# Beginning attention with half of the channels while the other half is still being measured

## Chip, cores and metric

The kernel runs on one core of a Trainium2 chip. The metric is the device time of one execution in microseconds (us). The engines are named as in the profile: PE (matrix products; PEld is its loading of weights), DVE (vector), ACT (scalar), POOL (GpSimd) and SP (which issues DMAs). Each engine has its own queue and works it in order; semaphores tie the queues together.

## What is computed

Four layers follow one another on a tensor of 512 channels by 64 x 64 pixels: an attention, two gated convolutions and a linear attention. Each takes its input through a group normalization and adds its result to it. Only the first matters here:

```python
x = x + _L0_conv_ref(_gn(x), wq, wk, wv, wo)

def _gn(v, G=32, eps=1e-5):          # groups of 16 channels, over all pixels
    m = mean of the group; s = variance of the group
    return (v - m) / sqrt(s + eps)

q = conv1x1(fmap, wq, gain_in); k = conv1x1(fmap, wk, gain_in); v = conv1x1(fmap, wv, gain_in)
sim = -(AA[:, :, None] + AA[:, None, :] - 2.0 * qk) * scale     # AA = sum(q * q)
out = softmax(sim) @ v
```

A group has 16 channels, so the statistics of channels 0 to 255 don't depend on those of 256 to 511.

## The kernel before

X, the input, lies in SBUF as four chunks of 128 channels by 4096 pixels, in eight blocks of 512 pixels. `trunk_kernel` loads it block by block (L171), chunks 0 and 2 by SP's queue and 1 and 3 by ACT's, 32 transfers of 256 KB. `_attention_pairs` then has DVE measure all 32 blocks (`bn_stats`, L568) and calls `_Norm.params` for all four chunks at once: DVE aggregates the statistics of a chunk (L95), PE multiplies with the mask `gmask`, which gives the mean of each group (L124), DVE makes `less`, the negative mean (L125), and the variance (L127 to L129), PE applies the mask again (L132), `known()` starts the shift of X's first block by the mean (`_Centered.take`, L383 on ACT and L385 on POOL or DVE), and DVE and ACT make the reciprocal root (L134 to L141). The reciprocal goes, as `gains` (L594, L595), into the weights instead of X (`_Centered.scaled`, L391 on ACT, L395 elsewhere).

`project(pair)` computes q, k and v for two heads (pair 0 and 2: also v for the next two). It works on two blocks of pixels at a time and is a loop of four rounds, k = 0 to 3. Each round has a "turned" half (`_SevenTurned`, the values v: X is the stationary operand, 16 matmul instructions of 128 columns in a product) and a direct half (`_Seven`, q and k: 4 instructions of 512 columns in a product). Each half uses a scheme of seven products where eight would be plain (`_Seven.steps`): sums of weights made once (`sums`, L441) and differences of blocks of X made each round (`differences`, L454), in four pairs that depend on one another in order. The steps come in the order p1, p5, p2, p7, p6, p3, p4. p1 multiplies chunks 0 and 1 of the first block with the first half of a weight, p2 chunks 2 and 3 with the second half. Both accumulate in one bank of PSUM, the memory that PE writes:

```python
def p1():
    add(0, a[:, 0:2], [x(c, 0) for c in range(2)], True)
    kept[0] = keep(0, ps[0])
def p2():
    add(0, a[:, 2:4], [x(2 + c, 0) for c in range(2)], False)
    put(0, 0, ps[0], None)
```

`keep` is an ACT copy to SBUF (L664), since p1 alone enters other sums too. `put` takes a result out: an ACT copy where nothing is added (L682), a DVE addition otherwise (L684). The additions of p7 and p6 into the kept sums are DVE's (L490, L494). At each round's end the squares of q are summed by PE (L671, tile ps_a). In round 0 of pair 0 the differences are pinned to program order on DVE.

PSUM banks for p1 and p5 come from a pool of three double banks (tag "s"), which the mask products (gn_ps), ps_a and later the scores share. Weights of pair 0 are loaded by SP inside `project` (L611), behind X in its queue. After pair 0's projection the attention of that pair begins (L745), then the other pairs, then the other layers.

The order of each engine's queue is made by a planner: it takes instructions by their place in the program where they are ready by its own estimate of time. `keep_in_program_order` pins an instruction behind the one traced before it on the same engine. The planner may move unpinned ones ahead: `step_b` (L1186), a small subtraction of the second layer that needs only the vector of biases, stands before the first statistic on DVE.

Of the kernel before, what the change touches and what calls it, by code (L numbers as in the profile page):

```python
# [10 lines left out]
FP = mybir.dt.float32  # L11
# [5 lines left out]
P = 128  # L17
# [4 lines left out]
BLK = 512  # L22
# [75 lines left out]
class _Norm:  # L98
# [3 lines left out]
    def __init__(self, nc, small, gmask, mv=None):  # L102
        self.nc, self.small, self.gmask = nc, small, gmask
        self.less = self.tile("less", NC)
        self.r = self.tile("r", NC)
        self.mv, self.given = mv, mv is not None
        if mv is None:
            self.mv = small.tile([P, NC, 2], FP, tag="gn_mv", name="gn_mv")

# [3 lines left out]
    def params(self, c0, c1, stats, bank, known=lambda: None):  # L113


        nc, n, mv, gmask = self.nc, c1 - c0, self.mv, self.gmask
        less, r = self.less[:, c0:c1], self.r[:, c0:c1]
        d, a, s, t = (self.tile(f"{v}{c0}", n) for v in "dast")
        if not self.given:
            for c in range(c0, c1):  # L120
                _aggregate(nc, mv, stats, c)
        yield
        ps = bank()
        nc.tensor.matmul(ps[:, 0:n], gmask, mv[:, c0:c1, 0], start=True, stop=True)  # L124
        nc.vector.tensor_scalar(less, ps[:, 0:n], -1.0, None, ALU.mult)  # L125

        nc.vector.tensor_add(d, mv[:, c0:c1, 0], less)  # L127
        nc.vector.tensor_mul(d, d, d)
        nc.vector.tensor_add(d, d, mv[:, c0:c1, 1])  # L129
        yield  # L130
        ps = bank()
        nc.tensor.matmul(ps[:, 0:n], gmask, d, start=True, stop=True)  # L132
        known()
        nc.vector.tensor_scalar(a, ps[:, 0:n], GN_EPS, None, ALU.add)  # L134
        nc.scalar.activation(s, a, AF.Sqrt)
        nc.vector.reciprocal(r, s)

        nc.vector.tensor_mul(t, r, r)
        nc.vector.tensor_mul(t, t, a)
        nc.vector.tensor_scalar(t, t, -0.5, 1.5, ALU.mult, ALU.add)  # L140
        nc.vector.tensor_mul(r, r, t)  # L141


def _all(pieces):
    for _ in pieces:
        pass
# [13 lines left out]
def trunk_kernel(ctx: ExitStack, tc: tile.TileContext, a: dict, out: bass.AP):  # L160
# [4 lines left out]


    X = base.tile([P, NC, N], FP, tag="X", name="X")
    for b in range(NB):
        for c in range(NC):
            eng = nc.sync if c % 2 == 0 else nc.scalar  # L170
            eng.dma_start(out=X[:, c, ts(b, BLK)], in_=a["x"][c, :, ts(b, BLK)])  # L171

    vec = base.tile([P, NVEC], FP, tag="vec", name="vec")
    nc.gpsimd.dma_start(out=vec, in_=a["vecs"])
# [38 lines left out]
    ]  # L213
    Z = dram.tile([NB, BLK], FP, tag="Z", name="Z")

    stats, mv = _attention(tc, a, X, ident, gmask, neg2, small, new_stats, centered)

    stats, norm = _gated_convs(tc, a, X, vcol, vall, gmask, small, new_stats, centered, stats, mv, F)
    _linear_attention(tc, a, X, vcol, vall, ident, gmask, small, centered, stats, norm, F3, Z, out)
# [134 lines left out]
class _Centered:  # L354
# [25 lines left out]
    def take(self, xs, c, eng=None):  # L380
        less = self.less[:, c : c + 1]
        if eng is None:
            self.nc.scalar.activation(xs, xs, AF.Identity, bias=less)  # L383
        else:
            eng.tensor_scalar(xs, xs, less, None, ALU.add)  # L385

    def scaled(self, w, rstd, eng, c0=0, c1=NC, pinned=False):

        if eng is self.nc.scalar:
            for c in range(c0, c1):  # L390
                eng.activation(w[:, c], w[:, c], AF.Copy, scale=rstd[:, c : c + 1])  # L391
# [28 lines left out]
class _Seven:  # L420
# [39 lines left out]
                skip_group_check=not first,  # L460
            )

    def steps(self, a, b, s, t, x, bank, keep, put, early=lambda more, last: None):

        nc = self.nc
        ps, kept = {}, {}

        def add(j, w, hs, first):  # L470

            if first:
                ps[j] = bank(j)
            self.multiply(ps[j], w, hs, first)

        def p1():
            add(0, a[:, 0:2], [x(c, 0) for c in range(2)], True)
            kept[0] = keep(0, ps[0])

        def p5():  # L480
            add(1, s[0], t[0], True)
            kept[1] = keep(1, ps[1])

        def p2():
            add(0, a[:, 2:4], [x(2 + c, 0) for c in range(2)], False)
            put(0, 0, ps[0], None)

        def p7():
            add(2, s[2], t[2], True)
# [36 lines left out]
SUM_LOW, SUM_HIGH = 1e-20, 1e30  # L526


def _attention_pairs(tc, a, X, QO, gmask, small, centered, stats, mv, okay):

# [18 lines left out]
    with tc.tile_pool(name="att1", bufs=1) as p1, tc.tile_pool(  # L549
# [16 lines left out]
        for b in range(NB):  # L566
            for c in range(NC):
                nc.vector.bn_stats(stats[:, c, b, :], X[:, c, ts(b, BLK)])  # L568
        norm = _Norm(nc, small, gmask)
        centered.by(norm)  # L570
        _all(
            norm.params(
                0, NC, stats, lambda: ps_mm.tile([P, BLK], FP, tag="mm", name="gn_ps"),
                centered.first(lambda c: X[:, c, 0:BLK]),
            )
        )
        rstd = norm.r


        halves = p1.tile([P, 32], FP, tag="halves", name="halves")  # L580
# [9 lines left out]
        A = p1.tile([P, NT, 2], FP, tag="A", name="A")  # L590


        gains = p1.tile([P, 2, NC], FP, tag="gains", name="gains")
        nc.vector.tensor_scalar(gains[:, 0], rstd, 2 * scale * gain_in, None, ALU.mult)  # L594
        nc.vector.tensor_scalar(gains[:, 1], rstd, gain_in, None, ALU.mult)  # L595
        seven = _Seven(tc, nc.tensor.matmul)

        turned = _SevenTurned(tc, nc.tensor.matmul)

        def home(pair):  # L600

            return V if pair % 2 else QO[NC - 1]
# [1 line left out]
        def project(pair, meanwhile=None):  # L604


            w = p1.tile([P, 3, NC, P], FP, tag="wqkv", name=f"wqkv{pair}")
            w = [w[:, n] for n in range(3)] + [p1.tile([P, NC, P], FP, tag="wo", name="wv")]
            src = [(pair, 0), (pair, 1), (pair, 2), (pair + 1, 2)][: 2 if pair % 2 else 4]
            for n, (p, m) in enumerate(src):  # L610
                nc.sync.dma_start(out=w[n], in_=a["L0_wqkv"][p][:, m])  # L611
            def scaled(n, eng, c0=0, c1=NC):
                centered.scaled(w[n], gains[:, n // 2 if n > 1 else n], eng, c0, c1, (pair, n, c0) == (0, 2, 0))

            if pair == 0:

                scaled(2, nc.vector, 0, 2)
                scaled(3, nc.scalar)
                scaled(0, nc.gpsimd)
                scaled(2, nc.vector, 2, NC)  # L620
                scaled(1, nc.scalar)
                centered.began()
            for n in range(len(src) if pair else 0):
                scaled(n, nc.gpsimd)
            Q = QO[pair]

            def matrices(t):
# [16 lines left out]
            def differences(k):  # L644
                if pair == k == 0:

                    return (
                        tc.keep_in_program_order(ins)
                        for ins in seven.differences(nc.vector, view(k), diff)
                    )  # L650
                if pair == 0:
                    for b in (2 * k, 2 * k + 1):
                        for c in range(NC if b else 0):
                            centered.take(X[:, c, ts(b, BLK)], c)
                return seven.differences(nc.vector, view(k), diff)

            def bank(j):
# [26 lines left out]
                    nc.vector.tensor_add(d, ps, more)  # L684

            late, psa = [], []
            for c in range(NC if pair == 0 else 0):
                centered.take(X[:, c, ts(1, BLK)], c)
            pieces = differences(0)
            for k in range(NB // 2):  # L690
                after = iter(())
                for g, (wa, wb, ws, sums) in enumerate(made):
# [2 lines left out]
                    steps = (turned if values else seven).steps(  # L695
                        wa, wb, ws, diff, view(k), bank, keep,
                        lambda m, n, ps, more: put(dst[m], 2 * k + n, ps, more),
                    )
                    for n, step in enumerate(steps):
                        if n == 0:  # L700
# [156 lines left out]
        nc.vector.tensor_scalar(okay, ps[0:1, 0:1], float(P), None, ALU.is_ge)  # L857


def _attention(tc, a, X, ident, gmask, neg2, small, new_stats, centered):  # L860

    nc = tc.nc
    gain_out = 1.0 / math.sqrt(C)
# [5 lines left out]
    _attention_pairs(tc, a, X, O, gmask, small, centered, stats, mv, okay)  # L869
    found = nc.values_load(okay[0:1, 0:1])  # L870
    with tc.If(found < 1, label="general"):

# [238 lines left out]
def _gated_convs(ctx, tc, a, X, vcol, vall, gmask, small, new_stats, centered, stats, mv, F):  # L1111
# [18 lines left out]
    for layer in ("L1", "L2"):  # L1130
# [55 lines left out]
        nc.vector.tensor_sub(step_b, b_in[:, :, 1], b_in[:, :, 0])  # L1186
        wsum = {}

        def more(n):
# [937 lines left out]
```

## Time and profile before

| what | value |
|---|---|
| runs | 3826.85, 3827.91 and 3833.11 us; median 3827.91 |
| profiled execution, span | 3828.3 us (TensorE clock granted: 0.996) |
| X transfers | 16 on ACT's queue, 16 on SP's; 5.4 and 5.5 us from issue to landing (median) |
| first statistic of X | 6.35 us |
| last aggregate done, gains made | 27.1, 31.6 us |
| first product of the projection | 33.06 us |
| first round ends, projection of pair 0 ends | 60.55, 136.5 us |

The page lists each engine's busy time and the span in 40 slices, one of them 96 us. The part that the change touches lies in the first slice and the beginning of the second, so it must be read from views of single stretches: the timeline (start, length, engine, line, operation, result and operands, and in brackets the idle time before and what ended it) and the table of busy times by stretch. A matmul's length in the timeline contains the pipeline; the distance between starts tells the pace.

### The profile page before, as it was taken

Reading aid. Unit: us, or ns where it says so; the run is one execution under the profiler, and the core shown is the slowest. Engines: PE = TensorE matmul, PEld = TensorE weight load, DVE = VectorE, ACT = ScalarE, POOL = GpSimd, SP = SyncE. Lnnn points to the kernel's source line nnn. Section 1 sums busy time; section 2 is a strip of 40 time slices with the busy share of each in tenths; the row PEclk is TensorE's granted clock in tenths of the full one; section 3 lists DMA queues with packets and bytes.
Section 4 is the critical chain, followed back from the end, with each engine's and each line's share of the span. In section 5 each row is a group of like instructions: output and inputs, shape, how many; then the busy total and the mean of one; then the engine's idle time right before and its main releaser. Section 6 shows DMA issues by size and latency. Waiting matters only on the chain. (4 is left out here: it accounts for less than half of the span.)

```text
span 3828.3 us, 81625 instructions
## 1 busy us (share of the span) xinstructions
PE 3752.0 (98%) x35294; PEld 1657.9 (43%) x35294; DVE 2688.1 (70%) x3242; ACT 2069.3 (54%) x2998; POOL 132.2 (3%) x112
## 2 busy tenths in 40 slices
PE   6999999999999999999999999999999999999999
PEld 5633334333365333343333334554445544455543
DVE  6577787777765777876776757766677677665437
ACT  3577774777735777746665655663246632355210
POOL 0000000000000000000000000000000000122112
PEclk9999999999999999999999999999999999999999
DMA  2000000000000000000000015772057730564312
GB/s 100 9 1 1 1 1 9 1 1 1 1 1 9 1 1 1 1 9 1 1 1 1 1 49 168 198 201 81 13 157 194 199 102 27 151 178 103 97 56 91
DMA packets 178413, 212.91 MB, mean 56 GB/s; under 512 B 13032, under 2 KB 121832, under 8 KB 177920
## 3 DMA queue, kind: packets, MB, share of 16 engines
q1 hardware_dynamic: 151232, 148.46, 14.5%
q10 hardware_dynamic: 26784, 59.11, 4.2%
q8 instruction: 280, 4.59, 0.5%
q14 instruction: 85, 0.70, 0.1%
q0 software_dynamic: 32, 0.06, 0.0%
HBM read 147.81 MB, written 59.77 MB: 54 GB/s over the span
## 5 line engine op out<-in xcount | busy, mean ns | idle before, releaser
L753 ACT ACTIVATE pt<-ps_s,A 128x512 f32<-128x512 f32 x2048 | 1286.3, 687 | 534.8 <-PE ps_s L745 527.1
L832 DVE TENSOR_TENSOR acc<-acc,pt 128x1024 f32<-128x1024 f32 x960 | 1174.1, 1223 | 327.8 <-ACT pt L753 300.8
L745 PE MATMUL ps_s<-O,K 64*64 64x512 f32 x8192 | 1111.6, 589 | 0.0
L745 PEld LDWEIGHTS ps_s<-O,K 64*64 64x64 f32 x8192 | 334.3, 133 | 553.8 <-issue 307.1
L765 PE MATMUL av<-pt,O 64*64 64x512 f32 x4096 | 558.2, 590 | 0.9 <-ACT pt L753 0.9
L765 PE MATMUL av<-pt,V 64*64 64x512 f32 x4096 | 554.4, 590 | 0.0
L1006 ACT COPY S<-S 32x1295 f32<-32x1295 f32 (+1 forms) x272 | 341.4, 1256 | 217.4 <-DMA S<-F 105.6
L765 PEld LDWEIGHTS av<-pt,O 64*64 64x64 f32 x4096 | 171.5, 133 | 276.1 <-issue 254.9
L765 PEld LDWEIGHTS av<-pt,V 64*64 64x64 f32 x4096 | 168.3, 133 | 281.0 <-issue 270.3
L933 PE MATMUL ps<-diff,w_sum 128*128 128x512 f32 x516 | 242.0, 601 | 3.1 <-DVE w_sum L441 1.9
L933 PEld LDWEIGHTS ps_cv<-S,T 64*32 64x32 f32 x13824 | 194.1, 105 | 111.5 <-issue 73.0
L933 PE MATMUL ps_cv<-S,T 64*32 64x128 f32 x13824 | 233.6, 273 | 5.0 <-issue 2.4
L933 PE MATMUL ps<-h,w_out_L 128*128 128x512 f32 x512 | 229.6, 599 | 1.5 <-DVE X L1287 1.4
L454 DVE TENSOR_TENSOR diff<-X 128x512 f32<-128x512 f32 x200 | 134.0, 683 | 83.1 <-PE ps L933 46.4
L383 ACT ACTIVATE X<-X,gn_less 128x512 f32<-128x512 f32 x122 | 77.3, 709 | 152.0 <-DVE gn_less L125 152.0
L933 PE MATMUL ps<-X,w_in_L 128*128 128x512 f32 x304 | 145.8, 611 | 10.8 <-ACT w_in_L L391 5.4
L933 PE MATMUL ps<-h,pw_L 128*128 128x512 f32 x320 | 143.8, 599 | 1.9 <-DVE h L1275 1.6
L933 PEld LDWEIGHTS ps<-h,w_out_L 128*128 128x128 f32 x512 | 94.0, 190 | 118.3 <-issue 96.5
L933 PEld LDWEIGHTS ps<-diff,w_sum 128*128 128x128 f32 x516 | 94.6, 190 | 116.8 <-issue 106.5
L454 DVE TENSOR_TENSOR diff<-X,diff 128x512 f32<-128x512 f32 x200 | 135.3, 683 | 12.9 <-PE ps L933 11.3
L1060 DVE STREAM_TRANSPOSE h<-ps_cv 128x512 f32<-128x512 f32 x112 | 109.2, 1048 | 48.6 <-PE ps_cv L933 48.2
L933 PE MATMUL ps<-agg,w_proj 128*128 128x512 f32 x256 | 118.5, 602 | 1.0 <-DVE turned L1060 0.9
(233 smaller groups left out, 3324.7 us busy)
## 6 DMA issues: line engine op xcount, KB each, us to landing
T<-in_L_T_dram SPq DMA_DIRECT2D x112, 384.0 KB, 4.6
F<-plane ACTq DMA_DIRECT2D x112, 324.0 KB, 3.5
S<-F SPq DMA_DIRECT2D x224, 162.0 KB, 4.6
S<-G SPq DMA_DIRECT2D x96, 153.0 KB, 4.3
G<-plane ACTq DMA_DIRECT2D x48, 289.0 KB, 2.5
row<-G SPq DMA_DIRECT2D x48, 272.0 KB, 3.3
T<-in_L_T_dram SPq DMA_DIRECT2D x48, 256.0 KB, 4.1
out_dram<-y SPq DMA_DIRECT2D x32, 256.0 KB, 2.0
```

The costliest lines, as they stand in the source:

```text
L383: self.nc.scalar.activation(xs, xs, AF.Identity, bias=less)
L454: yield eng.tensor_tensor(t[j][c], a(c), b(c), ALU.subtract)
L745: nc.tensor.matmul(ps[ts(half, D), ts(h, BLK)], K[rows, t * P + half * D : t * P + (half + 1) * D], QO[pair][rows, cols], start=True, stop ...
L753: exp = nc.scalar.activation(pt[:, ts(h, BLK)], ps[:, ts(h, BLK)], AF.Exp, bias=A[:, t, h : h + 1])
L765: nc.tensor.matmul(av[half][rows, :], v[keys, t * P + h * D : t * P + (h + 1) * D], pt[keys, ts(h, BLK)], start=(t == 0), stop=(t == NT - 1),)
L832: add = nc.vector.tensor_add(acc, acc if u > 1 else first, pt)
L933: self.tc.keep_in_program_order(self.nc.tensor.matmul(*args, **kw))
L1006: nc.scalar.copy(second, first)
L1060: nc.vector.transpose(out, src)
```

## The change

X is loaded in two parts: first chunks 0 and 1, on SP and ACT; then, after pair 0's four weights, chunks 2 and 3, all on SP. The statistics follow in that order, each pinned on DVE. The parameters are made twice, for chunks 0 and 1 and for 2 and 3. Within the first of these, a statistic of the second half is traced wherever the chain waits for another engine (`meanwhile`, and `pause` behind the root). Then the first halves of the weights are scaled, chunks 0 and 1 of blocks 0, 2, 4 and 6 are shifted (ACT and POOL by turns), and p1 of all four rounds, turned and direct, is done ahead (`begin`), eight products. Each result is copied by ACT into a part of QO[1], which pair 1 uses later. Four stand before the remaining statistics, three in the gaps of the second parameters, one after them. In the loop p1 takes p2's matmuls, alone in its bank, and adds the kept result on DVE; p2 does nothing. In addition ACT's root, copies and the scalings named in the diff are pinned, and `step_b` is pinned in both gated convolutions.

```diff
+    def load_x(chunks, engines):
+        for b in range(NB):
+            for c, eng in zip(chunks, engines):
+                eng.dma_start(out=X[:, c, ts(b, BLK)], in_=a["x"][c, :, ts(b, BLK)])
+
+    load_x((0, 1), (nc.sync, nc.scalar))
...
+        lambda: load_x((2, 3), (nc.sync, nc.sync)),
...
         nc.vector.tensor_scalar(a, ps[:, 0:n], GN_EPS, None, ALU.add)
-        nc.scalar.activation(s, a, AF.Sqrt)
+        self.pin(nc.scalar.activation(s, a, AF.Sqrt))
+        self.pause()
         nc.vector.reciprocal(r, s)
...
         def p1():
-            add(0, a[:, 0:2], [x(c, 0) for c in range(2)], True)
+            if p1_kept is not None:
+                kept[0] = p1_kept
+                add(0, a[:, 2:4], [x(2 + c, 0) for c in range(2)], True)
+                put(0, 0, ps[0], p1_kept)
+                return
+            ps[0] = bank(0)
+            self.first(a, x, ps[0])
             kept[0] = keep(0, ps[0])
...
         def p2():
-            add(0, a[:, 2:4], [x(2 + c, 0) for c in range(2)], False)
-            put(0, 0, ps[0], None)
+            if p1_kept is None:
+                add(0, a[:, 2:4], [x(2 + c, 0) for c in range(2)], False)
+                put(0, 0, ps[0], None)
...
+        def taken(b, c0, c1, engines=(None,)):
+            for c in range(c0, c1):
+                tc.keep_in_program_order(
+                    centered.take(X[:, c, ts(b, BLK)], c, engines[c % len(engines)])
+                )
+
+        def measure(b, c):
+            tc.keep_in_program_order(nc.vector.bn_stats(stats[:, c, b, :], X[:, c, ts(b, BLK)]))
+
+        first = [(b, c) for b in range(NB) for c in range(2)]
+        rest = [(b, 2 + c) for b, c in first]
...
+        def parameters(c0, c1, meanwhile, known):
+
+            norm.pause = meanwhile
+            for _ in norm.params(c0, c1, stats, bank_gn, known):
+                meanwhile()
+            for n, g in enumerate((2 * scale * gain_in, gain_in)):
+                nc.vector.tensor_scalar(gains[:, n, c0:c1], norm.r[:, c0:c1], g, None, ALU.mult)
...
+        for n in (2, 0, 3, 1):
+            load_w(n)
+        load_rest()
+        for at in first:
+            measure(*at)
+        parameters(
+            0, 2, lambda: measure(*rest.pop(0)), lambda: taken(0, 0, 2, (None, nc.gpsimd))
         )
-        rstd = norm.r
+        scaled_first(2, nc.scalar, 0, 2, True)
+        scaled_first(0, nc.gpsimd, 0, 2)
+        for k in range(1, NB // 2):
+            taken(2 * k, 0, 2, (None, nc.gpsimd))
...
+        def begin(n=1):
+
+            for _ in range(n):
+                k, values = to_begin.pop(0)
+                ps = ps_mm.tile([P, BLK], FP, tag="mm", name="ps7")
+                (turned if values else seven).first(
+                    w_first[2 if values else 0], lambda c, n: X[:, c, ts(2 * k + n, BLK)], ps
+                )
+                t = begun[k, values] = QO[1][:, ts(2 * k + values, BLK)]
+                tc.keep_in_program_order(nc.scalar.copy(t, ps))
+
+        begin(4)
+        for at in rest:
+            measure(*at)
+        parameters(2, NC, begin, lambda: taken(0, 2, NC, (nc.gpsimd, nc.vector)))
+        for n in (3, 1):
+            scaled_first(n, nc.scalar, 0, 2, True)
+        begin(len(to_begin))
...
             if pair == 0:
 
-                scaled(2, nc.vector, 0, 2)
-                scaled(3, nc.scalar)
-                scaled(0, nc.gpsimd)
-                scaled(2, nc.vector, 2, NC)
-                scaled(1, nc.scalar)
+                w = w_first
+                scaled_first(2, nc.vector, 2, NC, True)
+                scaled_first(3, nc.scalar, 2, NC, True)
+                scaled_first(0, nc.gpsimd, 2, NC)
+                scaled_first(1, nc.scalar, 2, NC, True)
                 centered.began()
...
+                        p1_kept=begun.get((k, values)) if pair == 0 else None,
...
-        nc.vector.tensor_sub(step_b, b_in[:, :, 1], b_in[:, :, 0])
+        tc.keep_in_program_order(nc.vector.tensor_sub(step_b, b_in[:, :, 1], b_in[:, :, 0]))
```

More of the change, by code (lines that the diff above doesn't have):

```diff
@@ L106, in __init__ @@
         self.mv, self.given = mv, mv is not None
+        self.pin = lambda ins: ins
+        self.pause = lambda: None
         if mv is None:
@@ L167, in trunk_kernel @@
     X = base.tile([P, NC, N], FP, tag="X", name="X")
[L168 to L171, printed above, removed]
+    def load_x(chunks, engines):
[3 more added lines that the diff above has]
+    load_x((0, 1), (nc.sync, nc.scalar))
     vec = base.tile([P, NVEC], FP, tag="vec", name="vec")
@@ L214, in trunk_kernel @@
     Z = dram.tile([NB, BLK], FP, tag="Z", name="Z")
-    stats, mv = _attention(tc, a, X, ident, gmask, neg2, small, new_stats, centered)
+    stats, mv = _attention(
+        tc, a, X, ident, gmask, neg2, small, new_stats, centered,
+        lambda: load_x((2, 3), (nc.sync, nc.sync)),
+    )
     stats, norm = _gated_convs(tc, a, X, vcol, vall, gmask, small, new_stats, centered, stats, mv, F)
@@ L382, in take @@
         if eng is None:
-            self.nc.scalar.activation(xs, xs, AF.Identity, bias=less)
-        else:
-            eng.tensor_scalar(xs, xs, less, None, ALU.add)
+            return self.nc.scalar.activation(xs, xs, AF.Identity, bias=less)
+        return eng.tensor_scalar(xs, xs, less, None, ALU.add)
     def scaled(self, w, rstd, eng, c0=0, c1=NC, pinned=False):
@@ L390, in scaled @@
             for c in range(c0, c1):
-                eng.activation(w[:, c], w[:, c], AF.Copy, scale=rstd[:, c : c + 1])
+                ins = eng.activation(w[:, c], w[:, c], AF.Copy, scale=rstd[:, c : c + 1])
+                if pinned:
+                    self.tc.keep_in_program_order(ins)
         else:
@@ L461, in multiply, with first, steps @@
             )
-    def steps(self, a, b, s, t, x, bank, keep, put, early=lambda more, last: None):
+    def first(self, a, x, ps):
+        self.multiply(ps, a[:, 0:2], [x(c, 0) for c in range(2)], True)
+    def steps(self, a, b, s, t, x, bank, keep, put, early=lambda more, last: None, p1_kept=None):
         nc = self.nc
@@ L526, with _attention_pairs @@
 SUM_LOW, SUM_HIGH = 1e-20, 1e30
-def _attention_pairs(tc, a, X, QO, gmask, small, centered, stats, mv, okay):
+def _attention_pairs(tc, a, X, QO, gmask, small, centered, stats, mv, okay, load_rest):
     nc = tc.nc
@@ L565, in _attention_pairs, with bank_gn @@
         nc.scalar.activation(mark, mark, AF.Sqrt)
-        for b in range(NB):
-            for c in range(NC):
-                nc.vector.bn_stats(stats[:, c, b, :], X[:, c, ts(b, BLK)])
+        def bank_gn():
+            return ps_mm.tile([P, BLK], FP, tag="mm", name="gn_ps")
+        def taken(b, c0, c1, engines=(None,)):
[3 more added lines that the diff above has]
+                )
@@ L569, in _attention_pairs @@
+        def measure(b, c):
+            tc.keep_in_program_order(nc.vector.bn_stats(stats[:, c, b, :], X[:, c, ts(b, BLK)]))
+        first = [(b, c) for b in range(NB) for c in range(2)]
+        rest = [(b, 2 + c) for b, c in first]
         norm = _Norm(nc, small, gmask)
+        norm.pin = tc.keep_in_program_order
         centered.by(norm)
[L571 to L575, printed above, removed]
-        )
@@ L577, in _attention_pairs @@
-        rstd = norm.r
+        gains = p1.tile([P, 2, NC], FP, tag="gains", name="gains")
+        def parameters(c0, c1, meanwhile, known):
[4 more added lines that the diff above has]
+                nc.vector.tensor_scalar(gains[:, n, c0:c1], norm.r[:, c0:c1], g, None, ALU.mult)
+        names = [(0, 0), (0, 1), (0, 2), (1, 2)]
+        w = p1.tile([P, 3, NC, P], FP, tag="wqkv", name="wqkv0")
@@ new lines, in _attention_pairs, with load_w, scaled_first @@
+        w = [w[:, n] for n in range(3)] + [p1.tile([P, NC, P], FP, tag="wo", name="wv")]
+        w_first = w
+        def load_w(n):
+            pair, m = names[n]
+            nc.sync.dma_start(out=w_first[n], in_=a["L0_wqkv"][pair][:, m])
+        def scaled_first(n, eng, c0=0, c1=NC, pinned=False):
+            centered.scaled(w_first[n], gains[:, n // 2 if n > 1 else n], eng, c0, c1, pinned)
+        for n in (2, 0, 3, 1):
[3 more added lines that the diff above has]
+            measure(*at)
@@ new lines, in _attention_pairs @@
+        parameters(
+            0, 2, lambda: measure(*rest.pop(0)), lambda: taken(0, 0, 2, (None, nc.gpsimd))
+        )
+        scaled_first(2, nc.scalar, 0, 2, True)
+        scaled_first(0, nc.gpsimd, 0, 2)
+        for k in range(1, NB // 2):
+            taken(2 * k, 0, 2, (None, nc.gpsimd))
+        seven = _Seven(tc, nc.tensor.matmul)
+        turned = _SevenTurned(tc, nc.tensor.matmul)
+        begun = {}
+        to_begin = [(k, values) for k in range(NB // 2) for values in (True, False)]
@@ new lines, in begin @@
+        def begin(n=1):
[4 more added lines that the diff above has]
+                    w_first[2 if values else 0], lambda c, n: X[:, c, ts(2 * k + n, BLK)], ps
+                )
+                t = begun[k, values] = QO[1][:, ts(2 * k + values, BLK)]
[3 more added lines that the diff above has]
+            measure(*at)
@@ L590, in _attention_pairs @@
         A = p1.tile([P, NT, 2], FP, tag="A", name="A")
[L593 to L598, printed above, removed]
         def home(pair):
@@ L604, in project @@
         def project(pair, meanwhile=None):
[L607 to L613, printed above, removed]
-            if pair == 0:
-                scaled(2, nc.vector, 0, 2)
-                scaled(3, nc.scalar)
-                scaled(0, nc.gpsimd)
-                scaled(2, nc.vector, 2, NC)
-                scaled(1, nc.scalar)
-                centered.began()
-            for n in range(len(src) if pair else 0):
-                scaled(n, nc.gpsimd)
+            if pair == 0:
+                w = w_first
[3 more added lines that the diff above has]
+                scaled_first(1, nc.scalar, 2, NC, True)
+                centered.began()
+            else:
+                w = p1.tile([P, 3, NC, P], FP, tag="wqkv", name=f"wqkv{pair}")
+                w = [w[:, n] for n in range(3)] + [p1.tile([P, NC, P], FP, tag="wo", name="wv")]
+                src = [(pair, 0), (pair, 1), (pair, 2), (pair + 1, 2)][: 2 if pair % 2 else 4]
+                for n, (p, m) in enumerate(src):
+                    nc.sync.dma_start(out=w[n], in_=a["L0_wqkv"][p][:, m])
+                for n in range(len(src)):
+                    centered.scaled(
+                        w[n], gains[:, n // 2 if n > 1 else n], nc.gpsimd
+                    )
             Q = QO[pair]
@@ L651, in differences @@
                 if pair == 0:
-                    for b in (2 * k, 2 * k + 1):
-                        for c in range(NC if b else 0):
-                            centered.take(X[:, c, ts(b, BLK)], c)
+                    if k:
+                        taken(2 * k, 2, NC)
+                    taken(2 * k + 1, 0, NC)
                 return seven.differences(nc.vector, view(k), diff)
@@ L686, in project @@
             late, psa = [], []
-            for c in range(NC if pair == 0 else 0):
-                centered.take(X[:, c, ts(1, BLK)], c)
+            if pair == 0:
+                taken(1, 0, NC)
             pieces = differences(0)
@@ L857, in _attention_pairs, with _attention @@
         nc.vector.tensor_scalar(okay, ps[0:1, 0:1], float(P), None, ALU.is_ge)
-def _attention(tc, a, X, ident, gmask, neg2, small, new_stats, centered):
+def _attention(tc, a, X, ident, gmask, neg2, small, new_stats, centered, load_rest):
     nc = tc.nc
@@ L868, in _attention @@
     mv = small.tile([P, NC, 2], FP, tag="mv", name="mv")
-    _attention_pairs(tc, a, X, O, gmask, small, centered, stats, mv, okay)
+    _attention_pairs(tc, a, X, O, gmask, small, centered, stats, mv, okay, load_rest)
     found = nc.values_load(okay[0:1, 0:1])
```

## The prediction

> **What bounds the kernel now.** I read the page first: PE is busy for 98% of the span, so what counts is when PE starts to have work and whether it then waits. The first of the 40 slices is the only one below 9. So I read the first 140 us: a table of stretches, the timeline, the waits and the DMA view.
>
> ```profile
> PE 3752.0 (98%) x35294; PEld 1657.9 (43%) x35294; DVE 2688.1 (70%) x3242; ACT 2069.3 (54%) x2998; POOL 132.2 (3%) x112
> PE   6999999999999999999999999999999999999999
> ```
>
> The stretches (length, then busy time of PE, PEld, DVE, ACT, POOL; the last columns are clock, DMA share and GB/s):
>
> ```profile
> 6.35:26.04 19.69, 0.00 (x0) 0.00 (x0) 19.39 (x33) 1.49 (x2) 0.00 (x0) 1.00 1.05 387
> 26.04:33.03 6.99, 1.15 (x4) 1.00 (x4) 5.05 (x21) 4.13 (x10) 2.88 (x2) 1.00 0.15 55
> 38.96:60.55 21.59, 21.59 (x121) 15.37 (x121) 12.45 (x22) 17.14 (x29) 0.00 (x0) 1.00 0.01 1
> 60.55:111.12 50.57, 50.57 (x297) 36.12 (x296) 23.45 (x37) 9.55 (x17) 0.00 (x0) 1.00 0.00 1
> ```
>
> Until 26 us DVE (statistics) and DMA (X) are both full; PE does nothing. From 26 to 33 a chain of small instructions makes means and gains. After it PE never stops. Timeline:
>
> ```profile
> 6.27 0.16 DVE L1186 TENSOR_TENSOR step_b<-vec 128x4 f32<-128x4 f32 x1 [4.35 <-DMA vec<-in_vecs_dram]
> 6.35 19.78 DVE L568 BATCH_NORM_STATS2 stats<-X 128x6 f32<-128x512 f32 x32
> ...
> 29.95 0.16 DVE L134 TENSOR_SCALAR gn_a<-gn_ps 128x4 f32<-128x4 f32 x1 [0.68 <-PE gn_ps L132]
> 31.47 0.16 DVE L595 TENSOR_SCALAR gains<-gn_r 128x4 f32<-128x4 f32 x1
> 33.06 3.76 PE L516 MATMUL ps<-wqkv,X 128*128 128x128 f32 x16 [3.15 <-ACT wv L391]
> 36.61 0.63 PE L516 MATMUL ps<-O,diff 128*128 128x128 f32 x2
> 37.04 1.92 PE L458 MATMUL ps<-X,wqkv 128*128 128x512 f32 x2
> 38.75 1.87 PE L516 MATMUL ps<-O,diff 128*128 128x128 f32 x14
> ```
>
> PE's first product starts at 33.06 and takes 3.4 us for 16 matmuls. Later ones, from PE's timeline, take 1.79 (turned, 112.91 to 114.69) and 1.72 us (direct, 126.11 to 127.83):
>
> ```profile
> 112.91 1.95 PE L516 MATMUL ps<-O,diff 128*128 128x128 f32 x16
> 114.69 1.95 PE L516 MATMUL ps<-wqkv,X 128*128 128x128 f32 x16
> 126.11 1.88 PE L458 MATMUL ps<-diff,w_sum 128*128 128x512 f32 x4
> 127.83 1.88 PE L458 MATMUL ps<-X,wqkv 128*128 128x512 f32 x4
> 136.50 0.64 PE L671 MATMUL ps_a<-sq,halves 128*32 128x256 f32 x8
> ```
>
> The loop's first round lasts 27.49 us (33.06 to 60.55), the next two 25.28 each, of which 0.57 is squares that the first lacks. So 27.49 - 24.71 = 2.8 us is lost at the start, and projection ends at 136.50.
>
> **What the Trainium skill says.** "TensorE: Matmul & The Clock Gate", "What's actually happening": PE runs at half clock until one busy window of about 3.4 us, and the window runs free of the kernel. The trace agrees: double pitch from 33.06 to 38.96, 5.9 us, hence the 2.8 lost (the granted clock in the table says 1.00 all the same). "DMA: Bandwidth & Descriptors", "Issuing engines are not separate DMA queues": SP and ACT share 16 DMA engines. Agrees: with both queues 387 GB/s; from 25.4 to 27 us, SP alone, slices of 328 to 451. "GPSIMD Engine Reference", "Specifications": POOL shares SBUF access with DVE instructions that have two SBUF inputs. Agrees: a 4-element multiply took 0.57 instead of 0.16 us beside POOL's 1.84 us shift of X. Statistics have one input, so I take them as undisturbed, an estimate.
>
> **The change part by part.**
>
> *Loads.* 256 KB at 387 GB/s is 0.68 us. The last of 32 X loads is issued at 19.90 and lands 5.4 later, so the n-th load lands near 3.4 + 0.68n. All new loads but eight go through SP, at 0.33 to 0.45 us of issue each, under 0.68: no new bound. Chunks 0 and 1 are in by n=16, 14.3 us; the four weights by 17.0 (they were last before); chunks 2 and 3 from 17.7 to 27.9 instead of 25.2. ACT is rid of eight issues.
>
> *step_b's pin.* DVE waited 4.35 us for vec before the first statistic. Now it starts with the first landing, 0.81 + 3.7 (the shortest from issue to landing in the view of tile X) = 4.5. DMA then paces it: the sixteenth ends at 15.0.
>
> *First parameters.* Two aggregates, 0.5: 15.6. Pinned behind them is a statistic of chunk 2's first block, which lands at 17.7. In-order DVE holds the mean there until 18.3 if the planner puts it ahead, and the shifts of X and the second mask product wait with it. Three small operations with 0.3 for contention: 19.1. From them to the variance 0.7 (29.26 to 29.95), the second statistic inside: 19.9. Root and third statistic: 20.6. Reciprocal to gains 1.25 (30.38 to 31.63): 21.9. First ACT scaling 0.4: **PE starts at 22.3**. Ends: 21.5 (mean ahead of the statistic), 23.5 (0.6 on each of two waits).
>
> *Eight products.* 4 x 1.79 + 4 x 1.72 = 14.0, plus the clock's start: half of 3.4 to 6.8 us, 1.7 to 3.4, I take 2.55. Two mask products for the second half stand in PE's queue, 0.5. Last early product: 22.3 + 2.55 + 14.0 + 0.5 = **39.35**. POOL's shifts (1.84 each, needed one per 3.5 us) and ACT's copies (0.59) lie beside it.
>
> *Second parameters.* DVE's 13 remaining statistics at 0.59: 21.9 + 7.7 = 29.6, aggregates 30.1. PE reaches their mask product only after the fifth early product, 22.3 + 2.55 + 8.8 = 33.6; the second mask product after the sixth, 35.6; gains 2.3 later (29.32 to 31.63), 38.0. So PE, not DVE, sets the pace, and the later landing costs nothing: its cover is the queue of products, 3.5 us thick.
>
> *Handover.* ACT's queue is pinned: copy of product 7, four scalings of 0.3, copy of product 8, then two scalings: 40.9. The sum of weights 0.4 (41.3), two differences 1.2 (42.5). The turned p1 on chunks 2 and 3 ends at 39.35 + 1.79 = 41.1: a hole of 1.4. p5 then ends at 44.3. p7, now next, needs the third pair of differences, and before these DVE does p1's add 0.6, three sums 1.1 and two other differences: 42.5 + 0.6 + 1.1 + 4 x 0.6 = 46.6: a hole of 2.3. Together 3.7. In the kernel before, the planner put half of the direct p1 into this very hole (37.04). If a whole one goes there, 1.7 is filled: **2.0** stays. Ends 0.5 and 3.7.
>
> *Rest of the loop.* Before, 136.50 - 33.06 - 2.8 = 100.6; without the early products 86.6. Eight ACT copies into the result (0.59) become DVE adds (0.69), and eight ACT copies of p1 go to the early phase. DVE is busy for 23.45 of 50.57 us in two rounds; four more adds of 0.69 make 26.2 of 43.6. I cost it at nothing, hidden by PE; if the cover fails, rival D. The other pins, the moved weight loads and the memsets: nothing, they are beside PE's work.
>
> **Sum.** 39.35 + 2.0 + 86.6 = 127.95, against 136.50: **8.55 us earlier**. After that PE is the bound in a stream that only shifts. The profiled execution spans 3828.3, 0.4 above the median of the runs (3827.9): 3828.3 - 8.55 - 0.4 = **3819.4**. What can be told from no change here is about 0.2%, 7.7 us; the forecast lies just past it. With all ends: gains of 4.8 to 11.7, so 3816.2 to 3823.1.
>
> **Rivals.**
> A. *Holes unfilled, late start*: the planner fills neither hole, PE starts at 23.5. 8.55 - 1.7 - 1.2 = 5.6: 3822.3. For it: DVE and ACT are pinned there. Against: it filled such a hole before.
> B. *All ends good*: mean goes first, clock warms soon, holes filled: gain 11: 3816.9. For: the wait for chunk 2 exists only if the planner believes it landed. Against: it needs luck in three places.
> C. *The mask product stands ahead of the early products in PE's queue.* PE then waits until 30.1 with most products undone, cools down and does them late: the end of product 8 moves from 39.35 to some 45.5: gain 2.4: 3825.5. For: the planner orders by its own times. Against: the products come first in the program.
> D. *Slower: evictions on DVE.* p1's bank is now freed by a DVE add in a queue with the differences, and with ps_a held only two such banks are left for p1 and p5. If the add stands behind a difference that waits for PE, the next block's p5 has no bank. It decides from a delay of one product plus one p1, 3.5 us; 2 us beyond that in each of eight blocks is 16: 3819.4 + 16 = 3835.4. For: DVE's queue is full after the fourth direct product. Against: per round it has about 13 of 21.8 us.
>
> **How the numbers follow.** Forecast 0.50, A 0.20, B 0.15, C 0.07, D 0.08. The forecast's own spread around 8.55 crosses 7.7: I count a tenth of it (0.05) as no change, and nothing of B. Faster 0.45 + 0.15 = 0.60, and 0.04 of A for a start in between: 0.64. No change 0.05 + 0.16 + 0.07 = 0.28. Slower 0.08. The range takes in A, B and the ends, 3815.5 to 3825.0; left out are D, most of C and tails.
>
> **What would show it.** First L516 product near 22, at double pitch for 3.4 to 6.8 us; the last early copy near 40; a few microseconds of PE gap or a direct product hoisted between 41 and 47; projection's last squares near 128; DVE's first statistic at 4.5 and a wait for DMA X between the aggregates and the mean. Wrong if: the first product comes after 25, PE waits on a mask product, or gaps of PE appear in rounds two to four.

## Result, and the profile after

The changed kernel takes 3820.44 us, the median of 7 runs (3817.9 to 3825.35); the kernel before, run beside it, 3831.18 (7 runs, 3826.85 to 3833.5). The ratio is 0.9975, 95% interval 0.9965 to 0.9985: 5.7 to 13.4 us faster. The profiled execution spans 3821.0 us, 7.3 less than that of the kernel before.

In the timeline of the changed kernel, the lines that answer to those of the prediction (start, length, engine, line, operation, tiles, and in brackets the idle time before and what ended it):

```profile
4.56 2.47 DVE L596 BATCH_NORM_STATS2 stats<-X 128x6 f32<-128x512 f32 x4 [2.64 <-DMA X<-in_x_dram]
...
15.27 0.58 DVE L95 BATCH_NORM_AGGREGATE gn_mv<-stats 128x2 f32<-128x48 f32 x2
...
17.71 0.69 DVE L596 BATCH_NORM_STATS2 stats<-X 128x6 f32<-128x512 f32 x1 [1.85 <-DMA X<-in_x_dram]
18.32 0.14 DVE L127 TENSOR_SCALAR gn_less<-gn_ps 128x2 f32<-128x2 f32 x1
...
22.51 0.80 PE L535 MATMUL ps<-wqkv,X 128*128 128x128 f32 x2 [2.41 <-ACT wqkv L398]
...
24.80 3.18 PE L535 MATMUL ps<-wqkv,X 128*128 128x128 f32 x14
```

The statistics start 1.8 us earlier. The first mean, `gn_less`, is made at 18.32 although its mask product began at 16.00: DVE stood for 1.85 us in front of the statistic ahead of it, whose block of X had not landed. PE starts at 22.51 instead of 33.06, at half pace.

The end of the early phase and the handover, on PE alone:

```profile
33.97 0.28 PE L126 MATMUL gn_ps<-gn_mv,gmask 128*128 128x2 f32 x2
...
36.05 2.03 PE L535 MATMUL ps<-wqkv,X 128*128 128x128 f32 x16
37.92 1.88 PE L467 MATMUL ps<-X,wqkv 128*128 128x512 f32 x4
39.64 1.95 PE L535 MATMUL ps<-wqkv,X 128*128 128x128 f32 x16
43.19 0.49 PE L535 MATMUL ps<-O,diff 128*128 128x128 f32 x2 [1.60 <-DVE diff L463]
43.51 1.02 PE L467 MATMUL ps<-X,wqkv 128*128 128x512 f32 x2
44.37 5.33 PE L535 MATMUL ps<-O,diff 128*128 128x128 f32 x46
...
128.00 0.64 PE L747 MATMUL ps_a<-sq,halves 128*32 128x256 f32 x8
```

Eight products lie between 22.51 and 39.64; then comes p1 of round 0, a hole of 1.76 us (p1's pace is 1.79, so 41.43 to 43.19), half of a direct p1 (43.51) as in the kernel before, and no further hole. Projection ends at 128.00 instead of 136.50. The table of stretches (length, then busy PE, PEld, DVE, ACT, POOL):

```profile
39.64:62.55 22.91, 21.31 (x121) 15.38 (x120) 17.08 (x31) 10.35 (x20) 0.00 (x0) 1.00 0.01 2
62.55:106.12 43.57, 43.57 (x257) 31.02 (x256) 25.46 (x41) 12.22 (x21) 0.00 (x0) 1.00 0.00 1
```

Rounds 1 and 2 last 43.57 us together instead of 50.57, and PE is busy throughout.

The 8.50 us are still there to a tenth when attention ends: its last exponential starts at 2212.65 instead of 2221.24, 8.59 earlier. In the layers behind it the distance wanders: 5.1 us at 2880 us, 8.1 at 3555, 7.3 at the end. So the experiments measure where projection ends, and the time of the whole kernel only where a version is to be judged.

### The profile page after: what moved, and what is told of

It is laid out like the page before. It is cut to its first block, busy times and chain, and to the rows that moved or that the text cites. A ratio compares the mean times of both kernels' runs of the same rounds, so it can differ in the third digit from the quotient of the medians.

```text
span 3821.0 us, 81661 instructions
## 1 busy us (share of the span) xinstructions
PE 3753.6 (98%) x35298; PEld 1658.8 (43%) x35298; DVE 2693.8 (70%) x3261; ACT 2063.6 (54%) x2989; POOL 138.5 (4%) x117
## 3 DMA queue, kind: packets, MB, share of 16 engines
q8 instruction: 280, 4.59, 0.5%
```

## Experiments

All numbers are starts from the trace of one profiled execution of each: the first early (or first) product, p1 of round 0 in the loop, which is where the last early product ends, p5 of round 0, and the end of projection, where the squares of its last round begin.

| run | first product | p1 in the loop | p5 | projection ends | from p1 to the end | against the change |
|---|---|---|---|---|---|---|
| before | 33.06 | | 36.61 | 136.50 | | +8.50 |
| changed | 22.51 | 39.64 | 43.19 | 128.00 | 88.36 | |
| e1: pin alone, on before | 33.09 | | 36.64 | 136.63 | | +8.63 |
| e2: none ahead | 32.78 | | 37.63 | 136.43 | | +8.43 |
| e3: old loads | 30.15 | 46.30 | 49.85 | 134.66 | 88.36 | +6.66 |
| e4: no statistics in the gaps | 20.44 | 37.54 | 41.08 | 125.90 | 88.36 | -2.10 |
| e5: two weights ahead | 21.35 | 38.14 | 41.68 | 126.50 | 88.36 | -1.50 |
| e6: PE kept busy | 22.29 | 36.99 | 40.53 | 125.35 | 88.36 | -2.65 |
| e7: ACT's order | 22.51 | 40.03 | 43.36 | 128.14 | 88.11 | +0.14 |
| e9: early shift | 22.48 | 39.83 | 42.41 | 127.16 | 87.33 | -0.84 |
| e10: early shift and ACT's order | 22.46 | 38.52 | 40.31 | 125.24 | 86.72 | -2.76 |
| e8: e5, no gaps, PE busy, e7 | 20.12 | 35.51 | 38.84 | 123.62 | 88.11 | -4.38 |
| e11: e8 and the early shift | 21.24 | 36.04 | 37.83 | 122.76 | 86.72 | -5.24 |

The last column can't be read alone. From the first product to the loop's p1 PE has the same work in the changed kernel, e4, e5, e7, e9 and e10, and yet it takes 17.13, 17.10, 16.79, 17.52, 17.35 and 16.06 us: the stretch at half pace at the start isn't equally long in each execution. A difference of 1 us in the last column can be that. The stretch from p1 to the end doesn't have this fault: it is 88.36 in all five kernels whose edit leaves the handover as it is, and equal in e7 and e8, and in e10 and e11. So an edit of the start is judged by the first product, one of the handover by this stretch. The times of whole kernels, one run each but for e8 and e11, don't help: e5's is the lowest of all, 3817.13, and e10's is 3823.52, although its projection ends 1.26 us earlier.

**e1, the pin of step_b alone**, put on the kernel before:

```diff
-        nc.vector.tensor_sub(step_b, b_in[:, :, 1], b_in[:, :, 0])
+        tc.keep_in_program_order(nc.vector.tensor_sub(step_b, b_in[:, :, 1], b_in[:, :, 0]))
```

> Kernel before with step_b's pin alone. Theory (DMA sets the end of the statistics): first statistic at 4.6 instead of 6.35 us, last one 0.3 us earlier at most, first product 32.8 to 33.1, projection of pair 0 ends at 136.2 to 136.5. Rival (DVE is the bound, the pin pays): everything 1.8 us earlier, end at 134.7.

```profile
7.53 10.57 DVE L568 BATCH_NORM_STATS2 stats<-X 128x6 f32<-128x512 f32 x16 [0.46 <-DMA X<-in_x_dram]
```

The first statistic starts at 4.59, the last at 25.48, where it was 25.45. The 1.8 us of early start are lost again to DMA: two waits for blocks of X take 0.63 of it, and for the rest the statistics follow one another more slowly, 0.66 us each in the line above against 0.6 before, close to the 0.68 at which blocks land. The pin pays nothing by itself; the rival is refuted.

**e2, no product ahead**, the rest as changed:

```diff
-        to_begin = [(k, values) for k in range(NB // 2) for values in (True, False)]
+        to_begin = []
-            for _ in range(n):
+            for _ in range(min(n, len(to_begin))):
```

> Changed kernel without the eight products ahead: p1 stays in the loop with p2, all else as changed. Theory (the products ahead are what pays): the two p1 of round 0 may still start near 22.5, as they need the first half alone; then PE waits for the second gains near 35 and for the sums, p5 near 37.7; projection ends near 138, ten later than changed and 1.5 later than before. Rival (the split of loads and statistics pays by itself): end at 128 to 130.

It ends at 136.43, as the kernel before. So the split of loads and parameters doesn't pay by itself, and on top of it the products ahead are worth all of the 8.4 us. The early start of p1 didn't come: p1 stood behind both mask products of the second half in PE's queue.

```profile
30.50 0.59 PE L126 MATMUL gn_ps<-gn_mv,gmask 128*128 128x2 f32 x2 [10.46 <-DVE gn_mv L95]
32.33 0.59 PE L134 MATMUL gn_ps<-gn_d,gmask 128*128 128x2 f32 x2 [1.24 <-DVE gn_d L131]
32.78 3.45 PE L535 MATMUL ps<-wqkv,X 128*128 128x128 f32 x16
37.63 0.49 PE L535 MATMUL ps<-O,diff 128*128 128x128 f32 x2 [1.40 <-DVE diff L463]
```

From there p1 ran beside the second parameters, at half pace, and PE then waited for p5, which came at 37.63 as expected (37.7), 1.0 later than in the kernel before. That the end is no later all the same, and most of the 1.6 us by which the guess of 138 was off, is the clock's doing: here PE was at full pace soon after p5 began, in the kernel before only from 38.96 on, and from p5 to the end it took 98.80 us instead of 99.89. At the same pace the split by itself would have cost about 1 us, an estimate from these two numbers.

**e3, X loaded as before**, products ahead as changed:

```diff
-    load_x((0, 1), (nc.sync, nc.scalar))
+    load_x(range(NC), 2 * (nc.sync, nc.scalar))
-        lambda: load_x((2, 3), (nc.sync, nc.sync)),
+        lambda: None,
```

> Changed kernel with X loaded block by block, all four chunks, by SP and ACT by turns, and the weights behind it. Theory (the load order lets the products start): first half complete at 23.8, first product near 31, projection ends near 136.5, no better than before. Rival (the order of loads hardly matters): end at 128 to 130.

First product 30.15, end 134.66: 1.8 better than before, where "no better" was expected. 0.85 of it is the start, which came that much before the 31 expected; about 1 us is the clock, as the early products took 16.15 us here and 17.13 in the changed kernel. Without the new order of loads at most 1.8 of 8.5 us are left, so loads and products ahead pay as a pair, and neither does alone.

**e4 and e5, the first mean's wait.** e4 traces no statistic of chunks 2 and 3 within the first parameters; e5 leaves it and loads two of the four weights behind X instead of all four ahead.

```diff
# e4
-            0, 2, lambda: measure(*rest.pop(0)), lambda: taken(0, 0, 2, (None, nc.gpsimd))
+            0, 2, lambda: None, lambda: taken(0, 0, 2, (None, nc.gpsimd))
# e5
-        for n in (2, 0, 3, 1):
-            load_w(n)
-        load_rest()
+        for n in (2, 0):
+            load_w(n)
+        load_rest()
+        for n in (3, 1):
+            load_w(n)
```

> Changed kernel with no statistic of chunks 2 and 3 in the gaps of the first parameters; they come after. Theory (the mean waits behind the statistic whose block lands at 17.7): mean at 16.5 instead of 18.3, first product near 21.0 instead of 22.5, projection ends near 126.5 instead of 128.0. Rival (the later statistics now end later and hold the second parameters): end at 128 or later.

> Changed kernel with only two of the four weights loaded ahead of chunks 2 and 3, the other two behind them. Theory (the mean waits for chunk 2's first block): that block lands two transfers, 1.35 us, earlier at 16.3; first product near 21.2, projection ends near 126.7. Rival (something else holds the start): no change, 128.0.

DVE in e4, then in e5:

```profile
16.46 0.16 DVE L127 TENSOR_SCALAR gn_less<-gn_ps 128x2 f32<-128x2 f32 x1 [0.74 <-PE gn_ps L126]
```

```profile
16.55 0.69 DVE L596 BATCH_NORM_STATS2 stats<-X 128x6 f32<-128x512 f32 x1 [0.59 <-DMA X<-in_x_dram]
17.16 0.14 DVE L127 TENSOR_SCALAR gn_less<-gn_ps 128x2 f32<-128x2 f32 x1
```

The mean moves from 18.32 to 16.46 and 17.16, the first product by 2.07 and 1.16, the end by 2.10 and 1.50; in e5 0.34 of the 1.50 is a shorter stretch at half pace. Theory holds in both: filling a gap of DVE with work whose data is not there yet makes the gap longer. e4's gain is 0.6 larger than expected. About half of that lies between the last aggregate and the gains, 4.24 us here (15.71 to 19.95) and 4.54 in the kernel before, where DVE also shifted a block of X; the rest wasn't followed up. What the rival feared didn't happen: without the stall DVE ends the second half's last aggregate at 30.21, where it was 30.50, although it has three statistics more to do after the gains. PE reaches their mask product at 31.87.

**e6, PE kept busy before the start.** 14 products of the mask with a block of X, whose result nobody reads:

```diff
+        spare = ps_av.tile([P, BLK], FP, tag="av0", name="spare")
+        turns = [9, 0, 3, 2]
+
+        def turn_over():
+            for _ in range(turns.pop(0)):
+                tc.keep_in_program_order(
+                    nc.tensor.matmul(spare, gmask, X[:, 0, 0:BLK], start=True, stop=True)
+                )
+        turn_over()
...
-            0, 2, lambda: measure(*rest.pop(0)), lambda: taken(0, 0, 2, (None, nc.gpsimd))
+            0, 2, lambda: (measure(*rest.pop(0)), turn_over()), lambda: taken(0, 0, 2, (None, nc.gpsimd))
```

> Changed kernel with 14 products of the mask with X, whose result nobody reads, on idle PE before the first early product. Theory (half clock costs 2.6 us at the start): early products at full pace from 22.5, the last ends near 37.0 instead of 39.6, projection ends near 125.4. Rival (the next bound, the second statistics near 30.5, takes most of it): end at 127 to 128.

```profile
19.72 1.96 PE L634 MATMUL spare<-X,gmask 128*128 128x512 f32 x4
22.29 2.18 PE L535 MATMUL ps<-wqkv,X 128*128 128x128 f32 x16 [0.61 <-ACT wqkv L398]
24.31 1.88 PE L467 MATMUL ps<-X,wqkv 128*128 128x512 f32 x4
```

The first product takes 2.0 us, where it took 3.4 at half pace in the kernel before; the last early one ends at 36.99, projection at 125.35. The 2.6 us are there: 2.43 from the early products (14.70 us instead of 17.13) and 0.22 from a first product that starts earlier. The second statistics don't take them back.

**e7, ACT's order at the handover.**

```diff
-        for n in (3, 1):
-            scaled_first(n, nc.scalar, 0, 2, True)
+        scaled_first(3, nc.scalar, 0, NC, True)
+        scaled_first(1, nc.scalar, 0, 2, True)
         begin(len(to_begin))
...
-                scaled_first(3, nc.scalar, 2, NC, True)
```

> Changed kernel with ACT's scaling of the second half of one weight ahead of the copy of the last early product. Theory (ACT's pinned order makes the hole of 1.7 us between p1 and p5): sum of weights 1.1 us earlier, hole 0.4, projection ends near 126.7. Rival (the next pair of differences makes a hole of its own): end at 127.7 or 128.0.

A miss: 128.14, or 0.25 gained from p1 to the end where 1.3 had been expected. ACT and DVE of this run show why:

```profile
40.76 0.57 ACT L652 COPY O<-ps 128x512 f32<-128x512 f32 x1
41.22 0.70 ACT L398 ACTIVATE wqkv<-wqkv,gains 128x128 f32<-128x128 f32 x2
41.82 2.55 ACT L391 ACTIVATE X<-X,gn_less 128x512 f32<-128x512 f32 x4
```

```profile
40.30 0.42 DVE L450 TENSOR_TENSOR O<-wv 128x256 f32<-128x256 f32 x1 [0.16 <-ACT wv L398]
...
42.02 0.69 DVE L759 TENSOR_TENSOR O<-ps,O 128x512 f32<-128x512 f32 x1 [0.37 <-PE ps L535]
42.62 1.32 DVE L463 TENSOR_TENSOR diff<-X 128x512 f32<-128x512 f32 x2
```

The same place in the changed kernel, DVE and then ACT:

```profile
41.04 0.43 DVE L450 TENSOR_TENSOR O<-wv 128x256 f32<-128x256 f32 x1 [1.29 <-ACT wv L398]
41.51 0.42 DVE L450 TENSOR_TENSOR O<-O,wqkv 128x256 f32<-128x256 f32 x1
41.85 0.68 DVE L760 TENSOR_TENSOR O<-ps,O 128x512 f32<-128x512 f32 x1
42.45 1.28 DVE L463 TENSOR_TENSOR diff<-X 128x512 f32<-128x512 f32 x2
```

```profile
41.50 2.54 ACT L391 ACTIVATE X<-X,gn_less 128x512 f32<-128x512 f32 x4
```

The sum of weights (40.30) is 0.74 earlier than in the changed kernel (41.04), but the difference that p5 needs still starts at 42.6. The weight sum isn't what ends last. Two other things do, close together. The difference reads block 1 of X, and that block's shift is ACT's, pinned behind all scalings and the copy; their number is the same in either order, and as one shift takes 0.71 us, ACT has shifted the first chunk at 42.53 here and at 42.21 in the changed kernel. And DVE has p1's addition (L759 here, L760 there) ahead of the difference; here it waited 0.37 us for p1's matmuls. So DVE is ready for the difference at 42.62 here, at 42.45 there.

**e9 and e10, block 1 shifted early.** It needs only the first half's mean, so POOL can do it while it is idle; e10 adds e7's order.

```diff
         for k in range(1, NB // 2):
             taken(2 * k, 0, 2, (None, nc.gpsimd))
+        taken(1, 0, 2, (nc.gpsimd,))
...
-                taken(1, 0, NC)
+                taken(1, 2, NC)
```

> Changed kernel with block 1 of chunks 0 and 1 shifted by POOL in the early phase, where POOL is idle, instead of by ACT after the last scalings; ACT's order otherwise as changed. Theory after the handover run (p5 waits for the difference, and that for ACT's shift of block 1, the last in ACT's pinned queue): the differences follow the weight sum, p5 starts at 42.1 to 42.6 instead of 43.2, projection ends near 127.2 instead of 128.0. Rival (weight sum alone holds p5): 128.0.

> The early shift and ACT's order of the handover run together. Theory (two waits end one behind the other, so only both together fill the hole): p5 starts near 41.6, right behind p1, projection ends near 126.5. Rival (the next differences make a hole of their own): 127.2 as with the shift alone.

DVE in e9, then PE in e10:

```profile
41.23 0.42 DVE L450 TENSOR_TENSOR O<-wv 128x256 f32<-128x256 f32 x1 [1.29 <-ACT wv L398]
41.58 1.29 DVE L463 TENSOR_TENSOR diff<-X 128x512 f32<-128x512 f32 x2
```

```profile
38.52 1.95 PE L535 MATMUL ps<-wqkv,X 128*128 128x128 f32 x16
40.31 2.00 PE L535 MATMUL ps<-O,diff 128*128 128x128 f32 x16
```

In e9 the difference follows the weight sum at once, p5 starts at 42.41, the end is 127.16: now the weight sum comes last, and it waits for ACT. In e10 p5 starts 1.79 us behind p1, which is p1's own pace: no hole. Its clock was also full sooner, so its last early product ends at 38.52 and not 39.83, which isn't the edit's doing. From there to the end of projection it is 88.36 in the changed kernel, 88.11 in e7, 87.33 in e9 and 86.72 in e10. So the hole was waits one behind the other: the early shift takes away 1.0, the earlier sum then another 0.6, but the earlier sum alone only 0.25. Without the clock's part e10 would end at 128.00 - 1.64 = 126.36, as expected.

The 1.0 isn't ACT's shift alone. With block 1 ready early the planner also puts the difference ahead of p1's addition on DVE, which stands at 42.78 in e9, behind both differences. The two are not separated by a run: in the changed kernel the addition let DVE go 0.24 us after the shift was there, so moving only one of them would have gained little.

**e8 and e11, the edits together**: no statistics in the gaps, two weights ahead, 12 unread products on idle PE, ACT's order; e11 with the early shift. Both were timed in seven runs.

> Two weights ahead, no statistics in the gaps, PE kept busy before the start, and ACT's order as in the handover run, together. Theory: first product near 21.0 at full pace, PE then waits some 0.8 us for the second statistics (30.5), last early product ends near 36.3, projection ends near 123.4, 13 us before the kernel before: ratio 0.9966, against 0.9975 of the change. Rival (the gains overlap): end at 125 or later.

> All four edits of the combined run and the early shift. Theory: the hole of 1.4 us closes there too, projection ends near 122.2 against 123.6, 14.3 us before the kernel before; in time a ratio near 0.9963. Rival (the shift on POOL, now beside the second statistics and differences, holds DVE): 123.6 or later.

Projection ends at 123.62 and 122.76 (expected 123.4 and 122.2). From p1 to the end it takes 88.11 and 86.72 us, as in e7 and e10: the handover's two steps come again, from another start. In e8 PE waits 0.46 us for the second statistics, where 0.8 had been expected: PE's queue no longer covers them. In time: e8 3822.43 us (7 runs, ratio 0.9971, 0.9960 to 0.9982), e11 3819.42 (7 runs, 0.9971, 0.9959 to 0.9982). Projection in e11 ends 5.2 us before that of the change, and yet the two can't be told apart in time: their intervals overlap for the most part. e8's median even lies 2 us above the change's, though each ran beside runs of its own of the kernel before. In its profile, 12.96 us against the kernel before are gained at the end of attention and 7.6 at the end of the kernel. Why the later layers give part of it back, and how much of that changes from one execution to the next, was not tried.

## Why the prediction was right

*Statistics and DMA.* The first statistic was put at 4.5 and came at 4.56. The load order's part, one landing each 0.68 us on SP alone, held: chunk 2's first block came at 17.7 as worked out.

*First parameters.* Mean at 18.3 (18.32), PE's start at 22.3 (22.51). The wait for chunk 2 that was named is the 1.85 in the line at 17.71; e4 removes it and e5 shortens it to 0.59, and the start moves with it.

*Eight products.* 14.0, 2.55 and 0.5 made 39.35; 39.64 was measured: 0.21 from the start, 0.28 for the two mask products, and 2.84 left for the clock. That the clock takes about this much is shown by e6, whose early products take 2.43 less. How much it takes in one execution is chance within the range that was given, 1.7 to 3.4: the same work took between 16.06 and 17.52 us in the runs above, which leaves 1.8 to 3.2 for the clock.

*Second parameters.* Mask product at 33.6 (33.97), gains at 38.0 (38.06). PE's queue covers the later statistics as worked out: their last aggregate ends at 30.50, 3.47 us before PE takes the mask product, where 3.5 had been said. e8, in which the early products start sooner and run faster, shows where the cover ends.

*Handover.* The size was right (2.0 against 1.76), the first half of the reason wrong. The step said that the sum of weights, followed at once by the differences, ends the wait of p5. In fact something else ended later: p1's addition and one more sum, which the planner had put ahead of the difference on DVE, and almost at the same time ACT's shift of block 1 (e7 against e9 and e10). The prediction had p1's addition behind the differences, and ACT's queue was counted up to the scaling that the sum needs, without the other two and the four shifts pinned behind it. p5 so began 0.7 later than worked out, and half a direct p1 (0.86), not a whole one, lay within it; its 14 last matmuls from 44.37 on end near 45.9 instead of 44.3. The third pair of differences was ready at 46.48, where 46.6 had been worked out, since DVE had the same work to do until then in whatever order. Matmuls of p6, whose differences were ready at 45.27, fill what is left, without a gap in the trace. The later p5 thus ate most of the second hole. That the sum came out is in part luck: the late operand was right, but a hole of 2.3 with a whole p1 put into it was worked out, and a longer first hole with other work in the second was found.

*Rest of the loop.* From p1 to the end it is 88.36, less the hole 86.60, where 86.6 had been worked out. A pair of rounds lost 7.0 us, the four products that left it: 43.57 against 50.57. Rival D, evictions on DVE, is refuted for this kernel: PE is busy for all of these 43.57 us, with DVE at 25.46 (26.2 was worked out).

*Sum.* 127.95 was predicted for the end of projection, 128.00 came, and the 8.5 us reached the end of attention. The time was put at 3819.4, from a median of three runs before (3827.91); over seven, before is at 3831.18. So the ratio, 0.9975, says 9.6 us and the sum 8.55, well within the interval. That the absolute time came within 1 us (3820.44) is luck: the starting value was 3.3 too low, and the medians lie 10.7 apart.

*Rivals A, B and C.* A's late start and B's mean ahead of the statistic didn't come, though A was half right about the first hole, which stayed open for 1.76 us; C is excluded by the line at 33.97, where the mask product follows the fifth early product.

## What to carry to other kernels

A normalization over groups can be begun with the part of the channels that is complete, but the order of loads and the work done ahead pay only together: here either alone gave 0.1 to 1.8 of 8.5 us. Before filling a gap of an in-order engine, ask whether the filler's data has landed; where it hasn't, the gap grows. Where a hole has a named cause, follow the late operand to the last instruction in the queue of the engine that makes it, look at what stands ahead of it in the queue of the engine that uses it, and test the cause by moving that one: two waits that end close to each other hide one another.

## What the runs showed of the hardware that was not expected

The time at half clock isn't a fixed price. PE starts at 22.46 in e10 and at 22.51 in the changed kernel, with the same work; yet the first early product is copied out at 26.91 in one and at 28.02 in the other. In e11 and e8 PE had nearly the same short work before the start, yet its last four unread matmuls took 3.38 us in e11 and 1.98 in e8:

```profile
18.07 3.38 PE L636 MATMUL spare<-X,gmask 128*128 128x512 f32 x4
21.24 2.29 PE L535 MATMUL ps<-wqkv,X 128*128 128x128 f32 x16
```

```profile
18.08 1.98 PE L636 MATMUL spare<-X,gmask 128*128 128x512 f32 x4
20.12 2.18 PE L535 MATMUL ps<-wqkv,X 128*128 128x128 f32 x16
```

In e11 the first 18 unread matmuls had ended sooner (14.44 against 15.58), so PE stood for 1.48 us before the mask product, and 0.34 in e8; the record of the clock has it at half from 18.5 on for 3.4 us, and the start came 1.1 us late. Whether the longer stand brought the clock down, or only the moment at which it came, no run separates. The tables of stretches of e11 and, below it, of the kernel before (the clock is the third number from the end):

```profile
18.50:21.90 3.40, 3.40 (x8) 1.67 (x7) 3.23 (x11) 2.25 (x5) 2.27 (x3) 0.50 1.06 388
```

```profile
33.03:38.96 5.93, 5.90 (x22) 4.89 (x22) 5.89 (x13) 4.12 (x9) 0.00 (x0) 1.00 0.00 0
```

The second line is a warning: there the record says full clock although the pace was half. Where the two differ, the distance between starts decides.

"TensorE: Matmul & The Clock Gate" in the Trainium skill, under "What's actually happening", says that the window in which activity is judged runs free of the kernel; these pairs agree with that, and don't prove it.

Statistics on DVE kept their 0.6 us pace beside POOL's shifts of X, as the prediction had only estimated. In the changed kernel, while POOL scaled a weight and shifted three blocks (22.03 to 27.28):

```profile
21.93 7.21 DVE L596 BATCH_NORM_STATS2 stats<-X 128x6 f32<-128x512 f32 x12
```

The contention that the prediction put in for instructions with two inputs is less regular than it says. During the same shift of X by POOL in the kernel before (28.09 to 29.93) one of them took 0.57 us, as it says, but two others took what they take elsewhere:

```profile
28.50 0.57 DVE L128 TENSOR_TENSOR gn_d<-gn_d 128x4 f32<-128x4 f32 x1
28.99 0.15 DVE L378 TENSOR_TENSOR offset<-offset,gn_less 128x4 f32<-128x4 f32 x1
29.10 0.16 DVE L129 TENSOR_TENSOR gn_d<-gn_d,gn_mv 128x4 f32<-128x4 f32 x1
```
